# Attention and 32 experts on one core: experts scatter weighted rows by token and choice instead of tokens gathering them

## The chip, the core and the metric

The kernel runs on one core of a Trainium2 chip. Its engines are TensorE (PE; the loads of its weights are PEld), VectorE (DVE), ScalarE (ACT), GpSimd (POOL) and SyncE (SP), which here only issues DMAs. The metric is device time in microseconds; lower is better. The kernel before took 1311.79 us, the median of three runs (1309.03 to 1314.77).

## What is computed

The input x has 8 sequences of 512 tokens with 128 channels, so N = 4096 tokens. A layer of causal attention (16 heads of 64, one null key and value for each head) is followed by a residual sum and a layer norm; the result is x1. Then comes a mixture of E = 32 experts, of which each token takes K = 4, and again a residual sum and a layer norm:

```python
w, idx = _gate(xf, wg)                       
fe = idx.reshape(-1)                         
pos = (jnp.cumsum(oh, axis=0) * oh).sum(-1) - 1
keep = pos < cap                             
dest = jnp.where(keep, fe * cap + pos, E * cap)
...
h = jax.nn.silu(jnp.einsum('ecd,edh->ech', xe, w1)) * jnp.einsum('ecd,edh->ech', xe, w3)
out = jnp.einsum('ech,ehd->ecd', h, w2) * buf_w.reshape(E, cap, 1)
y = jnp.zeros((N + 1, DIM), x.dtype).at[buf_tok].add(out.reshape(E * cap, DIM))[:N]
z = jax.nn.silu(xf @ sw1) * (xf @ sw3) @ sw2
return (y + z).reshape(shape)
```

There are 16384 choices and 20480 slots (32 x 640). A choice beyond the 640th of its expert is dropped; slots that nobody takes stay empty. Everything is float32.

## The kernel before

**Attention.** 64 steps, one for each sequence and pair of heads (g = 8 b + p). A step computes scores in four rounds of 128 queries (L462, two heads), adds the mask and takes the row minimum of the negated scores on VectorE (L472, into ns and nm), takes the exponential with its row sum on ScalarE (L482, into pr), and finishes with `normalize` (L488 to L501): on POOL pn is prepared (L492), ScalarE takes its exponential (L493), POOL adds it to the sums (L495), VectorE takes the reciprocal (L496), and POOL multiplies pr by it (eight L500). Two steps later pr is transposed on PE (L510; the copies out of PSUM are L515 on ScalarE and L517 on VectorE) and multiplied by v (L528; its copy yT is L536). The pool ps_m has four PSUM buffers; transposes, projections and outputs take turns on them. Score tiles have two buffers for each head.

**Routing.** When the eight pairs of a sequence are done, `finish` and `route` for this sequence are put piece by piece into the following steps: output projection (L257), norm (L283), transposed copy of x1 (L292, ScalarE), gate (L298), choice of groups and experts, positions by a product with a triangular matrix (L389, L390), and from these the slot of each choice, gidx (L403). Then `dispatch` issues 16 indirect DMAs for the sequence (L407, on POOL), one for each of 4 tiles and 4 choices. Each scatters 128 rows of 512 bytes from x1_all to their slots in xe_d in HBM. At the start SP's queue fills xe_d with zeros (L432).

The framework that builds the kernel tracks tiles: since all scatters write xe_d, each waits for the one before it to land. It also sets the order of the instructions on each engine, by its own schedule, within these dependencies. What is issued by POOL runs in that order, scatters and arithmetic alike.

**Experts.** The shared expert (L600 to L615) fills acc with x1 + z. Then for each of the 32 experts: SP loads its slots (xe, L625) and weights (L586), PE transposes five tiles of 128 slots (L633), multiplies by w1 and w3 (L600, L602) and w2 (L660), and SP stores the 320 KB result oe to oe_d (L668). The weights wait for the combination.

**Combination.** For each of 32 tiles of tokens and each of the four choices POOL gathers 128 rows of 512 bytes from oe_d (L678), and VectorE adds weight times row to acc (L684). After four tiles the layer norm's statistics are complete; POOL computes rstd (L691, L692), VectorE applies it (L695), and SP stores the result.

Of the kernel before, what the change touches and what calls it, by code (L numbers as in the profile page):

```python
# [17 lines left out]
P = 128  # L18
# [5 lines left out]
def attn_moe_kernel(  # L24
# [41 lines left out]
    xe_d = dram.tile([NSLOT, C], F32, name="xe_d")  # L66
    oe_d = dram.tile([NSLOT + 1, C], F32, name="oe_d")
# [3 lines left out]
    w_all = keep.tile([P, NTT, K], F32, name="w_all")  # L71
# [36 lines left out]
    zeros = const.tile([P, C], F32, name="zeros")  # L108
    nc.gpsimd.memset(zeros, 0.0)

# [7 lines left out]
    wat = astack.enter_context(tc.tile_pool(name="wat", bufs=1))  # L118
    ps_s = astack.enter_context(tc.tile_pool(name="ps_s", bufs=2, space=PSUM))
# [148 lines left out]

    def rstd_of(mv, name):
# [5 lines left out]
    def route(b, seq):  # L275
# [69 lines left out]

        def experts():
# [3 lines left out]
            for t in range(NT):  # L350
# [9 lines left out]
                w_all[:, t0 : t0 + NT, :], ev[:, :, :K], tot.unsqueeze(2).broadcast_to([P, NT, K]), ALU.mult  # L360
# [44 lines left out]
        def dispatch(t):  # L405
            for k in range(K):
                nc.gpsimd.indirect_dma_start(  # L407
                    out=xe_d[:, :],
                    out_offset=bass.IndirectOffsetOnAxis(ap=gidx[:, t0 + t, k : k + 1], axis=0),
                    in_=x1_all[:, t0 + t, :],  # L410
                    in_offset=None,
                    bounds_check=NSLOT - 1,
                    oob_is_err=False,
                )
# [4 lines left out]
        yield groups  # L419
        yield experts  # L420
# [10 lines left out]
    for z in range(0, NSLOT, P * ZR):  # L431
        nc.sync.dma_start(  # L432
            xe_d[z : z + P * ZR, :].rearrange("(p r) c -> p r c", r=ZR),
            zeros.unsqueeze(1).broadcast_to([P, ZR, C]),
        )
    nc.sync.dma_start(oe_d[NSLOT : NSLOT + 1, :], zeros[0:1, :C])
# [186 lines left out]
    def load_slots(e):  # L623
        xe = ework.tile([P, NJ, C], F32, tag="xe", name=f"xe_{e}")
        nc.sync.dma_start(xe, xe_d[e * CAP : (e + 1) * CAP, :].rearrange("(p j) c -> p j c", j=NJ))  # L625
        return xe

    def transpose_slots(e, xe):
        xeT = ework.tile([P, CAP], F32, tag="xeT", name=f"xeT_{e}")
        for j0, j1 in ((0, 4), (4, NJ)):  # L630
            px = ps_x.tile([P, 512], F32, tag="x", name=f"px_{e}_{j0}")
            for j in range(j0, j1):
                nc.tensor.transpose(px[:, (j - j0) * P : (j - j0 + 1) * P], xe[:, j, :], ident)  # L633
# [9 lines left out]
    for e in range(E):  # L643
# [4 lines left out]
        if e + 1 < E:  # L648
            xeTs[e + 1] = transpose_slots(e + 1, xes.pop(e + 1))
# [7 lines left out]
        for j0, j1 in ((0, 4), (4, NJ)):  # L657
# [5 lines left out]
            dst = oe[:, j0:j1, :].rearrange("p j c -> p (j c)")  # L663
            if j0 == 0:
                nc.scalar.copy(dst, po[:, : (j1 - j0) * C])
            else:
                nc.vector.tensor_copy(dst, po[:, : (j1 - j0) * C])
# [64 lines left out]
```

## Time and profile before

| | us |
|---|---|
| median of three runs | 1311.79 |
| the profiled execution, its own time | 1315.74 |
| its span on the core | 1314.0 |
| first slots to last slots scattered for the last sequence | 939.9 to 982.2 |
| first transpose of expert 0 | 986.3 |
| last store of an expert issued | 1120.9 |
| first gather | 1124.3 |
| last normalization ends | 1310.5 |

| engine | busy us | share of the span |
|---|---|---|
| PE | 1007.1 | 77% |
| DVE | 650.1 | 49% |
| ACT | 567.5 | 43% |
| POOL | 588.9 | 45% |

How to read it: the page divides the span into 40 equal slices (32.9 us each) and gives the busy share of each engine in tenths, 9 being 90% or more. A group's row has the line, the engine, the operation, the tiles it writes and reads, the number of instructions, then the busy time, the mean of one in ns, and the idle time of the engine just before them with what ended most of it. A timeline's row has start, duration, engine, line and operation, and in brackets the idle time before it and what ended that. "issue" means that the engine waited for nothing that the profile shows. The granted clock is TensorE's, 1.00 being full speed.

Further rows that the steps use: L407 has a median of 0.992 us and lies between 0.964 and 1.253; L500 takes 0.70 us for 512 columns; L515 0.57; L399 and L615 (128x512, VectorE) 0.69; the statistics L688 and L689 take 0.29 and 0.18; L692 1.04; the store of oe_d lands 2.4 us after its issue; the first slice moves 296 GB/s.

### The profile page before, as it was taken

How to read it: one execution, taken by the hardware profiler on the slowest of the kernel's cores; microseconds unless marked ns; L12 is line 12 of the kernel's file. 1: busy time of each engine (PE TensorE's matmuls, PEld its weight loads, DVE VectorE, ACT ScalarE, POOL GpSimd, SP SyncE). 2: the span in 40 equal slices, each digit the busy share in tenths (PEclk: the TensorE clock that was granted, in tenths of full speed). 3: DMA queues.
4: the chain of work that ended last, by engine and by line, in shares of the span. 5: the costliest groups of instructions: out<-in, count | busy, mean ns of one | idle time of the engine just before them, and what ended most of it. 6: DMA issues, size and time to landing. Idle time of an engine off the chain costs nothing.

```text
span 1314.0 us, 17689 instructions
## 1 busy us (share of the span) xinstructions
PE 1007.1 (77%) x5522; PEld 607.2 (46%) x5522; DVE 650.1 (49%) x2209; ACT 567.5 (43%) x1627; POOL 588.9 (45%) x1047
## 2 busy tenths in 40 slices
PE   6999998989899898999989899998809999100000
PEld 3555654655464464456446445655507777000000
DVE  3655573575557457455645745563604444233323
ACT  3676465546646555564655556553203444000000
POOL 0544356346535634653563465355130000576774
PEclk9999998989899898989989898999858999555555
DMA  9500000000000000000000000000016665121221
GB/s 296 154 1 1 9 13 21 1 11 21 11 9 13 21 1 11 23 9 9 15 18 2 5 21 9 1 14 19 14 32 192 211 211 168 59 65 48 64 59 45
DMA packets 62640, 62.69 MB, mean 48 GB/s; under 512 B 7337, under 2 KB 49746, under 8 KB 62546
## 3 DMA queue, kind: packets, MB, share of 16 engines
q1 hardware_dynamic: 54002, 44.25, 11.1%
q0 software_dynamic: 8192, 16.75, 4.4%
q8 instruction: 44, 0.72, 0.2%
q10 hardware_dynamic: 352, 0.55, 0.1%
q14 instruction: 50, 0.41, 0.1%
HBM read 30.11 MB, written 31.46 MB: 47 GB/s over the span
## 4 chain that ended last, share of the span: by engine, by line
PE 46%; POOL 20%; issue 13%; DVE 10%; DMA 6%; ACT 4%; another core or an unknown queue 1%; POOLq 0%; DVEq 0%; ACTq 0%; SPq 0%
PE y L528 8%; PE s L462 7%; POOL got L678 7%; PE t L510 6%; POOL pr L500 5%; POOL xe_d L407 5%; PE pm_o L257 4%; DMA xe_d<-x_all,gidx 4%; PE o L660 3%; PE pm_v L221 3%; ACT pr L482 3%; PE h L600 3%; PE h L602 3%; DVE ns L472 2%; PE pm_q L204 2%
## 5 line engine op out<-in xcount | busy, mean ns | idle before, releaser
L482 ACT ACTIVATE pr<-ns,nm 128x128 f32<-128x128 f32 (+3 forms) x512 | 283.5, 555 | 183.0 <-DVE nm L472 183.0
L472 DVE CUSTOM_DVE_ANT_0 ns<-s,mask,sn 128x128 f32<-128x128 f32 (+3 forms) x512 | 258.3, 546 | 117.8 <-PE s L462 96.7
L500 POOL TENSOR_SCALAR pr<-pr,tot 128x128 f32<-128x128 f32 (+3 forms) x512 | 265.6, 536 | 26.7 <-DVE tot L496 21.9
L462 PE MATMUL s<-k,q 64*128 64x128 f32 (+3 forms) x1024 | 210.3, 487 | 24.0 <-DVE nm L472 23.2
L678 POOL DMA_INDIRECT got<-oe_d,gidx x128 | 122.7, 959 | 179.0 <-issue 175.4
L528 PE MATMUL y<-prT,v 128*64 128x512 f32 (+3 forms) x1024 | 192.4, 469 | 6.8 <-DVE prT L517 6.8
L407 POOL DMA_INDIRECT xe_d<-x_all,gidx x128 | 129.2, 1009 | 138.5 <-DMA xe_d<-x_all,gidx 115.2
L510 PEld LDWEIGHTS t<-ident,pr 128*128 128x128 f32 x1280 | 141.0, 144 | 107.5 <-issue 55.0
L510 PE MATMUL t<-ident,pr 128*128 128x128 f32 x1280 | 185.7, 285 | 2.2 <-ACT yT L536 1.9
L462 PEld LDWEIGHTS s<-k,q 64*128 64x128 f32 x1024 | 80.9, 189 | 125.5 <-DVE nm L472 62.0
L528 PEld LDWEIGHTS y<-prT,v 128*64 128x64 f32 x1024 | 80.3, 144 | 117.4 <-issue 61.6
L492 POOL TENSOR_TENSOR pn<-nm,sn 128x8 f32<-128x8 f32 x64 | 16.1, 251 | 223.2 <-DVE nm L472 215.9
L515 ACT COPY prT<-t 128x512 f32<-128x512 f32 x192 | 108.6, 566 | 4.3 <-PE t L510 4.0
L482 ACT ACTIVATION_READ_ACCUMULATOR pr<-ns,nm 128x1 f32 x512 | 96.3, 188 | 0.0
L517 DVE COPY prT<-t 128x512 f32<-128x512 f32 x128 | 87.8, 686 | 14.0 <-PE t L510 10.1
L684 DVE SCALAR_TENSOR_TENSOR acc<-got,w_all,acc 128x128 f32<-128x128 f32 x128 | 44.0, 350 | 91.5 <-DMA got<-oe_d,gidx 64.7
L496 DVE RECIPROCAL tot<-tot 128x8 f32<-128x8 f32 x64 | 12.8, 200 | 143.2 <-POOL tot L495 143.2
L536 ACT COPY yT<-y 128x512 f32<-128x512 f32 x64 | 37.3, 583 | 104.5 <-PE y L528 104.5
L210 PE MATMUL pm_k<-xT,wk_sb 128*128 128x512 f32 x128 | 71.8, 645 | 2.2 <-ACT prT L515 1.7
L221 PE MATMUL pm_v<-wv_sb,xT 128*128 128x256 f32 x256 | 67.8, 395 | 0.0
L204 PE MATMUL pm_q<-xT,wq_sb 128*128 128x512 f32 x128 | 66.1, 598 | 2.0 <-ACT v L228 2.0
L257 PEld LDWEIGHTS pm_o<-wo_sb,yT 128*128 128x128 f32 x512 | 61.9, 192 | 7.8 <-issue 6.7
(133 smaller groups left out, 1126.2 us busy)
## 6 DMA issues: line engine op xcount, KB each, us to landing
xe_d<-zeros SPq DMA_DIRECT2D x8, 1280.0 KB, 11.4
xe<-xe_d SPq DMA_DIRECT2D x32, 320.0 KB, 3.4
oe_d<-oe SPq DMA_DIRECT2D x32, 320.0 KB, 2.4
w<-in_L_ffn_w_dram SPq DMA_DIRECT2D x96, 64.0 KB, 2.4
xn<-in_L_attn_x_dram SPq DMA_DIRECT2D x8, 256.0 KB, 4.8
xe_d<-x_all,gidx POOLq DMA_INDIRECT x128
got<-oe_d,gidx POOLq DMA_INDIRECT x128
out_dram<-ot SPq DMA_DIRECT2D x8, 256.0 KB, 2.3
```

What stands on the lines that cost most here:

```text
L204: nc.tensor.matmul(pm, wq_sb[:, p * P : (p + 1) * P], s["xT"], start=True, stop=True)
L221: nc.tensor.matmul(pm[:, t * 2 * P : (t + 1) * 2 * P], s["xT"][:, r * P : (r + 1) * P], wv_sb[:, c * 2 * P : (c + 1) * 2 * P], start=True, ...
L257: nc.tensor.matmul(pm[:, :C], s["yT"][p][:, rows], wo_sb[:, p, :], start=(p == 0), stop=False)
L407: nc.gpsimd.indirect_dma_start(out=xe_d[:, :], out_offset=bass.IndirectOffsetOnAxis(ap=gidx[:, t0 + t, k : k + 1], axis=0), in_=x1_all[:, ...
L462: nc.tensor.matmul(ps[e][:, :n], st["q"][e * D : (e + 1) * D, i * P : (i + 1) * P], st["k"][e * D : (e + 1) * D, :n], start=True, stop=True,)
L472: nc.vector.tensor_tensor_reduce(out=ns[:, :n], in0=ps[e][:, :n], in1=mask[:, T - n :], scale=1.0, scalar=s["sn"][:, i, 2 * p + e : 2 * p ...
L482: nc.scalar.activation(st["pr"][:, e, row0[i] : row0[i] + n], ns[:, :n], AF.Exp, bias=st["nm"][:, i, e : e + 1], scale=-1.0, accum_out=st[ ...
L500: nc.gpsimd.tensor_scalar(cols, cols, tot[:, i, e : e + 1], 1.0, ALU.mult, ALU.mult)
L510: nc.tensor.transpose(pt[:, k * P : (k + 1) * P], st["pr"][:, e, row0[i] + j * P : row0[i] + (j + 1) * P], ident)
L515: nc.scalar.copy(dst, pt)
L528: nc.tensor.matmul(yp[e * D : (e + 1) * D, j * P :], v[:, j, c0 : c0 + D], st["prT"][:, e, col0[j] : col0[j] + n], start=(j == 0), stop=(j ...
L678: nc.gpsimd.indirect_dma_start(out=got, out_offset=None, in_=oe_d[:, :], in_offset=bass.IndirectOffsetOnAxis(ap=gidx[:, n, k : k + 1], axi ...
```

## The change

Rows in xe_d grow from 128 to CE = 132 floats: behind the channels they carry the choice's own number (token x 4 + choice, as an integer) and its weight. ScalarE builds these rows in a new tile xk (four copies for each sequence), POOL writes the number, VectorE the weight. An empty slot carries a number that is out of bounds. The scatters of the dispatch are declared independent of each other, and the loads of xe get explicit dependencies on them.

The experts multiply by the weight when they copy out of PSUM: VectorE now takes the four-tile part, ScalarE the one-tile part. The store of oe is replaced by five indirect DMAs on POOL for each expert, which scatter 128 rows of 512 bytes each to y_d, at the row that the slot carries; out of bounds rows are not written. These too are declared independent. y_d is filled with zeros at the start. The combination waits for all of them, loads four contiguous rows for each token (1 MB for each group of four tiles), and adds them and acc; for every second group the widest add runs on POOL.

```diff
+    CE = C + 4
+    NOWHERE = 0x7F000000
+    xe_d = dram.tile([NSLOT, CE], F32, name="xe_d")
+    y_d = dram.tile([N * K, C], F32, name="y_d")
...
+    nc.gpsimd.memset(empty[:, C : C + 1].bitcast(I32), NOWHERE)
+    place = const.tile([P, NTT, K], I32, name="place")
+    nc.gpsimd.iota(place, pattern=[[P * K, NTT], [1, K]], base=0, channel_multiplier=K)
...
+    xkp = astack.enter_context(tc.tile_pool(name="xkp", bufs=1))
...
+    scatters = {"slots": [], "choices": []}
+
+    def apart(group, dma):
+
+        tc.declare_no_dep(dma.ins, group=group, reason="rows of its own")
+        tc.add_to_no_dep_group(group, dma.ins)
+        scatters[group].append(dma.ins.name)
+
+    def after(group, dma):
+
+        for name in scatters[group]:
+            tc.add_manual_dep(
...
+        def rows():
+
+            g["rows"] = xk = xkp.tile([P, NT, K, CE], F32, tag="xk", name=f"xk_{b}")
+            for t in range(NT):
+                nc.scalar.copy(
+                    xk[:, t, :, :C], x1_all[:, t0 + t, :].unsqueeze(1).broadcast_to([P, K, C])
+                )
+            nc.gpsimd.tensor_copy(xk[:, :, :, C].bitcast(I32), place[:, t0 : t0 + NT, :])
+            nc.gpsimd.memset(xk[:, :, :, C + 2 :], 0.0)
...
-                w_all[:, t0 : t0 + NT, :], ev[:, :, :K], tot.unsqueeze(2).broadcast_to([P, NT, K]), ALU.mult
+                g["rows"][:, :, :, C + 1], ev[:, :, :K], tot.unsqueeze(2).broadcast_to([P, NT, K]), ALU.mult
...
-                nc.gpsimd.indirect_dma_start(
-                    out=xe_d[:, :],
-                    out_offset=bass.IndirectOffsetOnAxis(ap=gidx[:, t0 + t, k : k + 1], axis=0),
-                    in_=x1_all[:, t0 + t, :],
...
+                apart(
+                    "slots",
+                    nc.gpsimd.indirect_dma_start(
+                        out=xe_d[:, :],
+                        out_offset=bass.IndirectOffsetOnAxis(ap=gidx[:, t0 + t, k : k + 1], axis=0),
+                        in_=g["rows"][:, t, k, :],
...
         yield groups
+        yield rows
         yield experts
...
-            zeros.unsqueeze(1).broadcast_to([P, ZR, C]),
+            empty.unsqueeze(1).broadcast_to([P, ZR, CE]),
         )
-    nc.sync.dma_start(oe_d[NSLOT : NSLOT + 1, :], zeros[0:1, :C])
+    ZR = 16
+    for z in range(0, N * K, P * ZR):
+        nc.sync.dma_start(
+            y_d[z : z + P * ZR, :].rearrange("(p r) c -> p r c", r=ZR),
+            zeros[:, :C].unsqueeze(1).broadcast_to([P, ZR, C]),
+        )
...
-        xe = ework.tile([P, NJ, C], F32, tag="xe", name=f"xe_{e}")
-        nc.sync.dma_start(xe, xe_d[e * CAP : (e + 1) * CAP, :].rearrange("(p j) c -> p j c", j=NJ))
+        xe = ework.tile([P, NJ, CE], F32, tag="xe", name=f"xe_{e}", bufs=5)
+        after("slots", nc.sync.dma_start(xe, xe_d[e * CAP : (e + 1) * CAP, :].rearrange("(p j) c -> p j c", j=NJ)))
...
-            if j0 == 0:
-                nc.scalar.copy(dst, po[:, : (j1 - j0) * C])
+            w = xes[e][:, j0:j1, C + 1 : C + 2]
+            if j1 - j0 == 1:
+                nc.scalar.activation(oe[:, j0, :], po[:, :C], AF.Copy, scale=w[:, 0, :])
             else:
-                nc.vector.tensor_copy(dst, po[:, : (j1 - j0) * C])
-        nc.sync.dma_start(oe_d[e * CAP : (e + 1) * CAP, :].rearrange("(p j) c -> p j c", j=NJ), oe)
+                nc.vector.tensor_tensor(
+                    oe[:, j0:j1, :],
+                    po[:, : (j1 - j0) * C].rearrange("p (j c) -> p j c", c=C),
+                    w.broadcast_to([P, j1 - j0, C]),
+                    ALU.mult,
+                )
+        xe = xes.pop(e)
+        for j in range(NJ):
+            apart(
+                "choices",
+                nc.gpsimd.indirect_dma_start(
+                    out=y_d[:, :],
+                    out_offset=bass.IndirectOffsetOnAxis(ap=xe[:, j, C : C + 1].bitcast(I32), axis=0),
+                    in_=oe[:, j, :],
+                    in_offset=None,
+                    bounds_check=N * K - 1,
+                    oob_is_err=False,
+                ),
+            )
...
+    y_t = y_d.rearrange("(n p k) c -> p n (k c)", p=P, k=K)
     for n0 in range(0, NTT, NT):
+        got = ework.tile([P, NT, K * C], F32, tag="got", name=f"got_{n0}", bufs=4)
+        after("choices", nc.sync.dma_start(got, y_t[:, n0 : n0 + NT, :]))
+        two = ework.tile([P, NT, 2 * C], F32, tag="two", name=f"two_{n0}", bufs=2)
+        half = nc.vector if (n0 // NT) % 2 == 0 else nc.gpsimd
+        half.tensor_tensor(two, got[:, :, : 2 * C], got[:, :, 2 * C :], ALU.add)
+        nc.vector.tensor_tensor(two[:, :, :C], two[:, :, :C], two[:, :, C:], ALU.add)
+        nc.vector.tensor_tensor(acc[:, n0 : n0 + NT, :], acc[:, n0 : n0 + NT, :], two[:, :, :C], ALU.add)
...
-            for k in range(K):
-                got = ework.tile([P, C], F32, tag="got", name=f"got_{n}_{k}", bufs=16)
-                nc.gpsimd.indirect_dma_start(
-                    out=got,
-                    out_offset=None,
-                    in_=oe_d[:, :],
-                    in_offset=bass.IndirectOffsetOnAxis(ap=gidx[:, n, k : k + 1], axis=0),
-                )
-                nc.vector.scalar_tensor_tensor(
-                    acc[:, n, :], got, w_all[:, n, k : k + 1], acc[:, n, :], ALU.mult, ALU.add
-                )
```

In the instruction order of the two builds, POOL's 16 scatters of a sequence stood in clumps of one to four among the instructions of `normalize` before, and stand in one row of 16 after; from the ninth on each waits for the one eight before it. On VectorE the reciprocal of the pair that follows them stood ahead of the next step's first two L472 before and stands behind them after. The pool of xk has one buffer; oe keeps three, xe gets five.

## The prediction

> **What bounds the kernel now.** I read the page's slices first, then its costliest groups, then the timelines of the stages that these point to. Slices 1 to 28 are attention, 29 and 30 the end of the dispatch, 31 to 34 the experts, 35 to 40 the combination.
>
> ```profile
> PE   6999998989899898999989899998809999100000
> ...
> POOL 0544356346535634653563465355130000576774
> ...
> L678 POOL DMA_INDIRECT got<-oe_d,gidx x128 | 122.7, 959 | 179.0 <-issue 175.4
> ...
> L407 POOL DMA_INDIRECT xe_d<-x_all,gidx x128 | 129.2, 1009 | 138.5 <-DMA xe_d<-x_all,gidx 115.2
> ...
> L496 DVE RECIPROCAL tot<-tot 128x8 f32<-128x8 f32 x64 | 12.8, 200 | 143.2 <-POOL tot L495 143.2
> ```
>
> PE is full in attention and in the experts and idle behind them: the last 190 us (1124.3 to 1314.0) belong to POOL's 128 gathers. Both indirect kinds hold POOL for about a microsecond each. The scatters also wait for one another (115.2 us), and VectorE waits for POOL (143.2 us, at the reciprocal of the softmax sums).
>
> POOL's timeline gives the two paces. First the last sequence's scatters, with nothing beside them, then gathers of the tail:
>
> ```profile
> 958.65 0.97 POOL L407 DMA_INDIRECT xe_d<-x_all,gidx  x1 [1.53 <-DMA xe_d<-x_all,gidx]
> 961.16 0.97 POOL L407 DMA_INDIRECT xe_d<-x_all,gidx  x1 [1.54 <-DMA xe_d<-x_all,gidx]
> ...
> 1143.07 0.94 POOL L678 DMA_INDIRECT got<-oe_d,gidx  x1 [0.30 <-issue]
> 1144.32 0.94 POOL L678 DMA_INDIRECT got<-oe_d,gidx  x1 [0.30 <-issue]
> ```
>
> A chained scatter takes 2.51 us (0.97 on POOL, 1.54 until it has landed). An unchained gather takes 1.25 (0.94 and a gap of 0.30). So an unchained scatter should take 0.97 + 0.30 = 1.27.
>
> What POOL's scatters do to attention is seen on PE's timeline in the middle of a batch:
>
> ```profile
> 670.76 1.02 PE L204 MATMUL pm_q<-xT,wq_sb 128*128 128x512 f32 x2
> 675.35 1.92 PE L462 MATMUL s<-k,q 64*128 64x384 f32 x4 [3.56 <-DVE nm L472]
> 677.19 1.11 PE L510 MATMUL t<-ident,pr 128*128 128x128 f32 x4
> 678.10 1.91 PE L210 MATMUL pm_k<-xT,wk_sb 128*128 128x512 f32 x2
> 679.94 2.08 PE L462 MATMUL s<-k,q 64*128 64x512 f32 x4
> 681.95 1.09 PE L510 MATMUL t<-ident,pr 128*128 128x128 f32 x8
> ```
>
> VectorE stood 8.19 us at the reciprocal, since four scatters were ahead of it on POOL; PE stood 3.56 us. Then PE ran at half speed: the four groups from 675.35 to 681.95 took 6.60 us, and the same four a step earlier 3.35, so 3.25 were lost as well. The clock row by stage shows the same (granted 0.93 from 178.8 to 230.0, 1.00 from 60.0 to 126.7).
>
> **The change, part by part.** The sum is against the profiled execution: 1315.74 us, of which 1314.0 are span. It lies 3.95 above the median of the runs, 1311.79; I take the difference over to the median.
>
> *Attention, sequences 0 to 6.* The chain between scatters goes: in the built order each waits only for the one eight before it. But the scheduler now issues all 16 of a sequence in a row, where they stood before in clumps of one to four between the normalizations. I follow sequence 4's times. The slots are ready at 637.4; 16 x 1.27 hold POOL until 657.7. The head pair behind them needs POOL (L492), ScalarE's exponential, POOL (L495) and VectorE's reciprocal, by their rows 1.5 us: 659.2. ScalarE stands at that exponential and VectorE at that reciprocal, which the new order puts behind two ns of the next step; that step's scores start at 645.9. PE can go on through two rounds of scores, eight transposes, a q, a third round and four transposes: by the rows from 645.9 to 650.0. Then PE lacks a PSUM buffer, because ScalarE has not copied the first transposes. ScalarE must first do four pr (0.4 to 0.5 and 0.19 each) and that copy (0.57), so PE resumes at about 661.9. It stands 11.9 us and then loses the 3.25 at half speed: 15.2. What the clumps cost before: from the five yT copies after the slots, the steps of sequence 0 take 9.82, 13.72, 14.95, 12.61 and 10.68, and without a dispatch 9.82, 11.16, 10.68, 11.16 and 10.68, so 8.3. Net +7.0 for each of seven sequences: **+49**. Bounds: if nothing of the clump reaches PE, -8.3 each; if all of the 20.3 does, with the slow clock, +15.
>
> *Rows that carry destination and weight.* Four ScalarE copies (128x512, 0.57 by the row of L515) for each sequence. ScalarE has a gap of 1.33 us just there; three of the four come ahead of the x1T copy, on which PE already waits 1.1 us. I take 0.4 x 8 = **+3**. POOL's small writes are issued in its idle time. Zeroing y_d adds eight stores of 1 MB on SP's queue, ahead of the experts' weights and the fourth sequence's x; these are needed from 290 us on, the fills end near 100, and the first scatter waits for them only at 180: nothing. If that cover were gone, 8.4 MB at the 296 GB/s of the first slice are 28 us.
>
> *Dispatch of the last sequence.* It is on the path: 939.9 to 982.2. Unchained 16 x 1.27 - 0.3 = 20.0: **-22**.
>
> *Experts.* Now 4.07 us each, PE full (granted clock 1.00 from 995 to 1116). Behind each expert POOL gets five scatters in place of SP's one store: 5 x 1.28 = 6.4 us (a little over 1.27, since scatters beside VectorE have a median of 0.99). POOL becomes the bound. From the first transpose to the first store are 8.9 us, with the wider multiply 9.2; then 160 x 1.28 = 204.8; then 1.5 until the last has landed: 215.5, against 137.9 from the same point to the first gather: **+78**. Three oe and five xe buffers give two experts' slack, so that POOL doesn't starve: expert e may write its oe once the scatters of e-3 have landed, some 12 us ahead of its turn. Behind that wait stand VectorE's and ScalarE's work for the next expert, behind the reload of xe on SP the next weights; both are then early by the same slack. The multiply takes VectorE's 0.69 in place of 0.29, beside POOL. Bounds of one scatter: 0.97 + 0.17 (the smallest gap) = 1.14 and 1.06 + 0.30 = 1.36, the far end 2.51.
>
> [...]
>
> *Combination.* 128 gathers, 128 multiply-adds and eight stops for rstd go (189.7 us). In their place come eight 1 MB loads, which wait for all scatters; behind them on SP are only the output stores. First landing: 1.05 MB at 296 GB/s is 3.5, and 2.4 as a 320 KB store takes: 6. VectorE then has for each group of four tiles two adds of 512 (0.69 each by L399), eight statistics (2.1), four normalizations (1.2), and in every second group the wide add (1.4): 43 in all; the last rstd on POOL adds 1.5, fill 1.5: 46. The other seven loads (25 us) lie beside it, as do POOL's four wide adds (at least 1.4 by L500). After the last normalization come 3.5, as now. 6 + 46 + 3.5 = 55.5 against 189.7: **-134**. Bounds 45 and 70.
>
> Sum: 49 + 3 - 22 + 78 - 134 = -26, and with the roundings -27: 1289 in that execution, **1285** by the median.
>
> **Rivals.**
> 1. *The clump costs attention no more than the scattered ones did.* PE has run ahead before: 8.19 us of VectorE's standing cost it only 3.56. Then the 49 go and 1236 is left (1178, if nothing of it reaches PE). Against it: ScalarE is held too, and PSUM has four buffers of that kind.
> 2. *The scatter is slower among the experts* (the slower side). The place is POOL's 160 scatters; the price is 160 us for each microsecond. It decides at (1312 - 1285) / 160 = 0.17 over 1.28, that is 1.45. At 1.6 the kernel takes 1336, at the chained 2.51 (if the declared independence did not hold) 1482. For it: rows grow and their source is read beside VectorE and ScalarE; two such gathers took 1.09. Against it: the built order shows waits eight back, and gathers beside VectorE held 1.25.
> 3. *PE stays at half speed among the experts.* It would be busy 4.07 of 6.4 us. At half speed it needs up to 8.1: 32 x 1.7 = 54 more, 1339. It decides above 7.2 us for an expert. Against it: pauses are 2.3 us, and a PE that is slow is always busy, which in this trace ends the slow state after 6.6 us.
>
> On this the row above shows the half speed after a pause of 3.56 us. [...]
>
> **How the numbers follow.** Forecast 0.56, 1260 to 1308 by the near bounds; first rival 0.14 (1236, with 0.03 of it wholly hidden); second 0.16 (over 1311); third 0.06; the clump's full price (15 in place of 7, 1341) 0.08. The range 1236 to 1324 reaches to the first rival and into the slower ones. Over 0.5% is 6.6 us, about what a measurement can tell from no change. Faster: nearly all of the forecast, the first rival and a little of the third, 0.71; same 0.08; slower 0.21.
>
> **What would show it.** Scatters among the experts 1.25 to 1.30 apart and POOL full there; PE idle 10 to 13 us once in each sequence, released through ScalarE; the last sequence's scatters 1.27 apart; about 55 us from the last scatter to the end. I would be wrong if scatters came 1.45 apart or more, if PE showed no such pauses, or if loads or adds stretched the end beyond 70 us.

## The result, and the profile after

The changed kernel takes **1327.17 us** (median of five runs, 1322.64 to 1330.39), beside 1311.79 for the kernel before (1309.03 to 1314.77). The ratio is 1.0118 [1.0086, 1.0151]: 1.2% longer, which is clear of the noise but under 2%, where 1285 and a range of 1236 to 1324 were forecast.

From the profile's page of the changed kernel, the slices and three of the costliest groups:

```profile
PE   6999987996999699879969996997884666676500
...
POOL 0534355426433643554274346435414666666633
PEclk9999998987998799989879997989886878778855
...
L722 POOL DMA_INDIRECT y_d<-oe,xe x160 | 155.4, 971 | 95.8 <-issue 53.3
...
L445 POOL DMA_INDIRECT xe_d<-xk,gidx x128 | 125.8, 983 | 70.8 <-issue 38.2
...
L541 DVE RECIPROCAL tot<-tot 128x8 f32<-128x8 f32 x64 | 13.0, 203 | 139.2 <-issue 64.4
```

The row of nines that PE had in attention is broken by a 6 or 7 once per sequence. The experts are slices 32 to 38 in place of four, with PE at 5 to 7 and POOL at 6, not at the 7 or 8 that scatters 1.28 apart would give (0.97 / 1.28 = 0.76). The tail is two slices in place of six. The scatters of the dispatch (L445) no longer wait for each other, and a scatter among the experts holds POOL for 0.971 us, one of the dispatch for 0.983.

The profiled execution took 1330.39 us (span 1328.6), the one before 1315.74 (1314.0). By the stages of the two timelines:

| stage | before | after | difference | forecast |
|---|---|---|---|---|
| start to the last sequence's first scatter | 939.9 | 992.9 | +53.0 | +49 + 3 |
| that sequence's dispatch | 42.3 | 22.0 | -20.3 | -22 |
| from its last scatter to the end of the experts' stage | 142.1 | 252.6 | +110.5 | +78 |
| from there to the end of the span | 189.7 | 61.2 | -128.5 | -134 |
| sum | 1314.0 | 1328.6 | +14.6 | -27 |

The cuts are at 939.9, 982.2 and 1124.3 (the first gather) before, and at 992.93, 1014.88 and 1267.45 (the last scatter has landed) after. Of the miss of about 41 us, 32.5 are in the experts.

**The clump in attention** is as the prediction drew it. A timeline of the changed kernel, end of a row of 16 scatters:

```profile
692.06 0.97 POOL L445 DMA_INDIRECT xe_d<-xk,gidx  x1 [0.30 <-issue]
693.30 0.21 ACT L538 ACTIVATE pn<-pn 128x8 f32<-128x8 f32 x1 [12.13 <-issue]
693.82 0.20 DVE L541 RECIPROCAL tot<-tot 128x8 f32<-128x8 f32 x1 [10.63 <-issue]
...
695.50 1.22 PE L218 MATMUL pm_k<-xT,wk_sb 128*128 128x512 f32 x1 [10.76 <-DVE prT L562]
```

POOL comes to the normalization only after its last scatter; ScalarE has stood 12.13 us by then and VectorE 10.63; PE, which waits for a copy out of PSUM behind them, 10.76.

**In the experts** the surprise is visible at PE's results. The changed kernel's timeline, with the columns start, duration, engine, line and, in brackets, the idle time before it and what ended that:

```profile
1030.40 0.94 PE L705 MATMUL o<-w,hT 128*128 128x128 f32 x6
1031.15 0.69 DVE L712 TENSOR_TENSOR oe<-o,xe 128x512 f32<-128x512 f32 x1 [0.81 <-issue]
...
1035.71 0.94 PE L705 MATMUL o<-w,hT 128*128 128x128 f32 x6 [1.23 <-issue]
...
1039.43 0.97 POOL L722 DMA_INDIRECT y_d<-oe,xe  x1 [0.30 <-issue]
...
1041.49 0.69 DVE L712 TENSOR_TENSOR oe<-o,xe 128x512 f32<-128x512 f32 x1 [5.83 <-remote]
1041.53 0.37 ACT L710 ACTIVATE oe<-o,xe 128x128 f32<-128x128 f32 x1 [7.42 <-remote]
...
1042.17 0.97 POOL L722 DMA_INDIRECT y_d<-oe,xe  x1 [1.77 <-issue]
```

VectorE's group over all 32 experts:

```profile
L712 DVE TENSOR_TENSOR oe<-o,xe 128x512 f32<-128x512 f32 x32 | 22.1, 691 | 112.5 <-remote 63.9 <-PE h L645 19.4 <-PE o L705 9.9
```

At 1031.15 VectorE takes PE's result o at once. The next o is done at 1036.65 at the latest by PE's records, but VectorE and ScalarE start on it at 1041.5, 4.8 us later. "remote" says that nothing in the profile released them. The moment is telling: POOL's last scatter before the pause left it at 1040.40, and 1.1 us later, when a scatter lands (its semaphore is raised at 1041.50), both results arrive. Then POOL, which had run dry, starts again: a gap of 1.77 us. It is no single case: of VectorE's 17 oe that come over 1.5 late, 15 start 1.03 to 1.22 us after POOL's last scatter ended.

The trace also records the semaphores, counters that one engine's instructions raise and another's wait for. PE's, on which this oe waits, is raised at 1035.08 and then not before 1041.46, though eight matmuls that raise it have ended by their records in between; the DMA that this oe waited for as well had landed at 1022.49. And it is the third expert's oe in three buffers, so no earlier scatter held it. What ended the wait was PE's late signal.

I call a result late by the time from the later of two moments to its consumer's start: the recorded end of the matmul that the consumer waits for, and the end of its engine's instruction ahead (for oe also the landing of the scatters that held its buffer, for VectorE's L649 the end of ScalarE's L648, whose result it multiplies). The usual value is 0.04 to 0.15, the largest of the kernel before 0.48. After the change 61 of the experts' 256 results are over 0.5 late, the latest 7.4. The scatters are 1.276 apart where they follow each other, as forecast, but 19 gaps, one for about every second expert, hold 34.2 us. With them the mean spacing is 1.49.

**In the tail** a timeline of the changed kernel shows two of the eight groups' ends, without and with POOL's wide add beside them:

```profile
1279.96 1.11 DVE L753 TENSOR_SCALAR ot<-acc,mv,rstd 128x128 f32<-128x128 f32 x4 [0.94 <-POOL rstd L750]
...
1286.29 2.34 POOL L740 TENSOR_TENSOR two<-got 128x1024 f32<-128x1024 f32 x1
1286.35 3.13 DVE L753 TENSOR_SCALAR ot<-acc,mv,rstd 128x128 f32<-128x128 f32 x4 [1.24 <-POOL rstd L750]
```

Four normalizations take 3.13 us beside POOL's add and 1.11 otherwise.

### The profile page after: what moved, and what is told of

Read it like the earlier page. It is cut to its first block, busy times and chain, and to the rows that moved or that the text cites. A ratio compares the mean times of both kernels' runs of the same rounds, so it can differ in the third digit from the quotient of the medians.

```text
span 1328.6 us, 18045 instructions
## 1 busy us (share of the span) xinstructions
PE 1050.8 (79%) x5522; PEld 639.2 (48%) x5522; DVE 641.4 (48%) x2101; ACT 576.1 (43%) x1659; POOL 626.5 (47%) x1102
## 4 chain that ended last, share of the span: by engine, by line
PE 59%; issue 14%; DVE 8%; another core or an unknown queue 6%; POOL 5%; ACT 5%; DMA 2%; SPq 0%; POOLq 0%; DVEq 0%; ACTq 0%
PE y L573 12%; PE s L507 11%; PE t L555 9%; PE pm_o L265 4%; PE pm_v L229 4%; PE pm_q L212 4%; PE pm_k L218 3%; ACT pr L527 3%; PE o L705 3%; DVE ns L517 2%; PE h L647 2%; PE h L645 2%; POOL pr L545 2%; PE px L678 1%
## 5 line engine op out<-in xcount | busy, mean ns | idle before, releaser
L545 POOL TENSOR_SCALAR pr<-pr,tot 128x128 f32<-128x128 f32 (+3 forms) x512 | 262.0, 531 | 26.5 <-DVE tot L541 20.3
L507 PE MATMUL s<-k,q 64*128 64x128 f32 (+3 forms) x1024 | 214.1, 484 | 12.8 <-DVE tot L541 9.8
L573 PE MATMUL y<-prT,v 128*64 128x384 f32 (+3 forms) x1024 | 198.6, 469 | 5.0 <-DVE prT L562 3.6
L722 POOL DMA_INDIRECT y_d<-oe,xe x160 | 155.4, 971 | 95.8 <-issue 53.3
L445 POOL DMA_INDIRECT xe_d<-xk,gidx x128 | 125.8, 983 | 70.8 <-issue 38.2
L573 PEld LDWEIGHTS y<-prT,v 128*64 128x64 f32 x1024 | 84.6, 144 | 109.9 <-issue 55.2
L218 PE MATMUL pm_k<-xT,wk_sb 128*128 128x512 f32 x128 | 72.9, 654 | 64.9 <-DVE prT L562 54.0
L705 PE MATMUL o<-w,hT 128*128 128x128 f32 x320 | 63.6, 343 | 72.0 <-DVE hT L649 46.9
L562 DVE COPY prT<-t 128x512 f32<-128x512 f32 x128 | 87.9, 687 | 19.6 <-PE t L555 19.4
L581 ACT COPY yT<-y 128x512 f32<-128x512 f32 x64 | 37.5, 585 | 137.1 <-PE y L573 122.9
L705 PEld LDWEIGHTS o<-w,hT 128*128 128x128 f32 x320 | 53.5, 240 | 89.0 <-DVE hT L649 52.9
L712 DVE TENSOR_TENSOR oe<-o,xe 128x512 f32<-128x512 f32 x32 | 22.1, 691 | 112.5 <-remote 63.9
L710 ACT ACTIVATE oe<-o,xe 128x128 f32<-128x128 f32 x32 | 11.7, 367 | 148.4 <-remote 76.5
```

Source lines behind the costliest of these rows:

```text
L218: nc.tensor.matmul(pm, wk_sb[:, p * P : (p + 1) * P], s["xT"], start=True, stop=True)
L445: nc.gpsimd.indirect_dma_start(out=xe_d[:, :], out_offset=bass.IndirectOffsetOnAxis(ap=gidx[:, t0 + t, k : k + 1], axis=0), in_=g["rows"][ ...
L507: nc.tensor.matmul(ps[e][:, :n], st["q"][e * D : (e + 1) * D, i * P : (i + 1) * P], st["k"][e * D : (e + 1) * D, :n], start=True, stop=True,)
L545: nc.gpsimd.tensor_scalar(cols, cols, tot[:, i, e : e + 1], 1.0, ALU.mult, ALU.mult)
L562: nc.vector.tensor_copy(dst, pt)
L573: nc.tensor.matmul(yp[e * D : (e + 1) * D, j * P :], v[:, j, c0 : c0 + D], st["prT"][:, e, col0[j] : col0[j] + n], start=(j == 0), stop=(j ...
```

## The experiments

The kernels of a group ran on one chip; I: e1 to e4, II: e5 to e8, III: e9 to e12, IV: e13 to e16, V: e17 and e18. The record numbers these chips 6, 0, 1, 8 and 0 again. Before on them took 1301.62, 1312.77, 1315.41, 1316.5 (one run) and 1297.7. Where no other base is named, a diff is against the changed kernel.

### Group I: buffers, pace, chain, plain stores

The first theory (A) was that PE's results are late because of the scatters beside them; rival B was that the buffers of oe and xe run out.

**e1, more buffers.**

```diff
-        xe = ework.tile([P, NJ, CE], F32, tag="xe", name=f"xe_{e}", bufs=5)
+        xe = ework.tile([P, NJ, CE], F32, tag="xe", name=f"xe_{e}", bufs=8)
-        oe = ework.tile([P, NJ, C], F32, tag="oe", name=f"oe_{e}")
+        oe = ework.tile([P, NJ, C], F32, tag="oe", name=f"oe_{e}", bufs=6)
```

> Six buffers for oe in place of three and eight for xe in place of five; nothing else. In the profile of the changed kernel POOL stands 1.5 to 2.2 us longer than its usual 0.30 ahead of about every second expert's first scatter, about 34 us over 32 experts. Theory A: these gaps come from TensorE's results reaching VectorE and ScalarE late (up to 7 us after the matmul's end) while a row of independent scatters runs on POOL; buffers do not help, the gaps stay within 34 +- 8 us, and the time stays at 1318 to 1330. Theory B: the gaps come from oe and xe buffers that are released by the scatters' landing; with more of them the gaps go, and the time is about 1327 - 34 = 1293.

Measured: 1291.83 (1291.57 to 1295.8), 0.9929 [0.9904, 0.9954]. POOL has no gaps, the experts take 218.3 (1014.89 to 1233.14, when the last scatter has landed). Groups of the trace of e1:

```profile
L712 DVE TENSOR_TENSOR oe<-o,xe 128x512 f32<-128x512 f32 x32 | 22.1, 692 | 26.3 <-PE o L705 19.4 <-DMA y_d<-oe,xe 7.0
...
L722 POOL DMA_INDIRECT y_d<-oe,xe x160 | 155.5, 972 | 61.5 <-issue 33.5 <-ACT xeT L682 13.0 <-DMA y_d<-oe,xe 9.1
```

VectorE now waits for PE's o and never for "remote". By itself this speaks for B; but no result is late in attention either (in its rows of 16 the changed kernel had 17), where e1 changes nothing. So the run could also owe it to the chip or the time at which it ran, and that had to be tried again (e5, e7).

**e2, a pause between scatters:** a multiply of 128x256 on POOL ahead of each scatter of the experts.

```diff
+        op = nc.gpsimd.tensor_scalar(idle, idle, 1.0, None, ALU.mult)
...
         for j in range(NJ):
+            pause()
             apart(
```

> Ahead of each of the experts' 160 scatters POOL does one multiply of an idle 128x256 tile. POOL's L500 took 0.70 us for 512 columns in the kernel before, so some 0.4 us each, and a scatter every 1.7 to 1.8 us instead of 1.28: 160 x 0.45 = 72 us more on POOL. Theory A1 (the lateness of TensorE's results depends on the rate of the scatters): no result comes more than 0.5 us late, the gaps between the experts go, and the time is about 1327 + 72 - 34 = 1365. Theory A2 (it depends on how many independent scatters have run since POOL's last pause, about seven): results are late by several us as before, gaps stay, 1395 to 1405. Theory B (buffers) says nothing on lateness.

Measured: 1428.26, 1.0964 [1.0919, 1.1009]. No result is late, but none was late in e1 and e3 either. The pause cost more than thought: the spacing is 2.11, not 1.7 to 1.8, and 160 x 0.83 = 133 us.

**e3, the dispatch of sequences 0 to 6 chained again,** the last one's left independent.

```diff
-                apart(
+                (apart if b == B - 1 else lambda group, dma: scatters[group].append(dma.ins.name))(
```

> The dispatch of sequences 0 to 6 is chained again (each scatter waits for the one before it to land, as in the kernel before, and the built order spreads them again in clumps of one to three); the last sequence's 16 scatters stay independent. In the profile the last sequence's first scatter starts at 992.9 against 939.9 before. Theory C (the clumps of 16 on POOL cost this): it starts at 940 to 946, and the time is 1327 - 50 = 1277. Rival (the four row copies on ScalarE and the filling of y_d cost it): it stays near 990 and the time near 1325.

Measured: 1254.29 (1249.36 to 1264.7), 0.9619 [0.9575, 0.9663], 37.5 less than e1 on its chip. In the profiled run, the longest of the four, the last sequence's first scatter comes at 960.9, not at 940 to 946, against 992.94 in e1. So the clump in attention costs more than the whole change loses, and a chain that spreads the scatters between normalizations is worth it. e3 has the three and five buffers of the changed kernel, and here POOL has no gaps among the experts either, which speaks against B already.

**e4, plain stores** in place of the experts' scatters.

```diff
-                nc.gpsimd.indirect_dma_start(
-                    out=y_d[:, :],
...
+                nc.gpsimd.dma_start(
+                    y_d[(e * NJ + j) * P : (e * NJ + j + 1) * P, :], oe[:, j, :]
```

> The experts' five scatters are plain stores of the same 64 KB, issued by POOL as well and independent as well, to consecutive rows of a longer y_d: this kernel leaves out that each row goes to its own place. Theory A-indirect (TensorE's results are late only beside indirect DMAs): no result is over 0.5 us late, no gaps; if a plain store holds POOL as long as a scatter (1.28), the time is about 1293, and less if it holds it shorter. Theory A-any (late beside any row of DMAs that POOL issues): late by several us, gaps as before, 1327 at the same spacing.

Measured: 1217.13, 0.9352 [0.931, 0.9393]. That is 75 less than e1: about what 160 indirect scatters cost over 160 stores where no result is late (e4 has the smaller buffers).

### Group II: the same kernel again, and the dispatch spread out

**e5, the changed kernel unchanged.**

> The changed kernel itself, unchanged, beside kernels of its own kind. Before took 1301.6 in the last experiments, where no result of TensorE came late in the runs with more buffers and with chained dispatch, 1311.8 when the changed kernel was timed. Theory A-place (the late results belong to the chip or the moment in which the changed kernel was timed, not to the kernel): if before takes some 1300 again, no result is over 0.5 us late, the gaps on POOL are gone with the three and five buffers that it has, and the time is that of the run with more buffers, 1292 (0.993 of before). Theory B (more buffers removed the gaps): gaps of about 34 us again, 1.0118 of before.

Measured: 1329.23 (1327.13 to 1333.02), 1.0129 [1.01, 1.0157]. 61 late results, gaps of 37.2, and 17 late in attention. The loss comes back.

**e6, the dispatch spread:** single scatters, each ordered behind the last POOL instruction of the normalization ahead of it, four behind each of four.

```diff
+        if group == "slots" and len(normalized) < B * NP:
+            tc.add_manual_dep(
+                dma.ins,
+                normalized[-1],
+                mybir.DependencyInfo(mybir.DependencyClass.NoSync, mybir.DependencyReason.DATA),
...
-            yield lambda t=t: dispatch(t)
+            for k in range(K):
+                yield lambda t=t, k=k: dispatch(t, k)
```

> All scatters of the dispatch stay independent, but for sequences 0 to 6 four of them are ordered behind each of four normalizations, in place of 16 in a row. Four scatters take 5.1 us of POOL, a step's normalization about 4.9, a step 10.7 to 11.2. Theory C (the row of 16 is what stretches attention): the last sequence's first scatter comes at 940 to 950 (992.9 in the changed kernel, 960.9 with the chain), and the time is the changed kernel's of the same chip less 43 to 53. Rival D (POOL then has no room, and each of these steps stretches as with the chain): 960, and the changed kernel's time less 32.

Measured: 1245.31 (1240.66 to 1248.26), 0.9498 [0.9464, 0.9532]; the last sequence's first scatter comes at 899.7. The time is 84 less than that of e5, where 43 to 53 were expected. Windows from 135 to 240 us, a sequence with its dispatch: first of the kernel before, then of the changed one, then of e6. The columns are length, busy time of PE, PEld, DVE, ACT and POOL with their instructions, granted clock, DMA share and GB/s.

```profile
135.00:240.00 105.00, 96.35 (x530) 54.56 (x529) 58.68 (x212) 57.78 (x170) 53.15 (x103) 0.95 0.04 14
```

```profile
135.00:240.00 105.00, 90.97 (x515) 53.60 (x514) 55.71 (x204) 55.95 (x163) 49.67 (x99) 0.93 0.04 14
```

```profile
135.00:240.00 105.00, 101.73 (x585) 59.13 (x584) 64.34 (x232) 65.42 (x190) 56.46 (x113) 1.00 0.04 14
```

In the same 105 us e6 gets 585 matmuls done, before 530, after 515, and only in e6 is the granted clock 1.00. The five steps behind the slots take 53.51 on average, against 61.40 before, 67.32 after, and 53.50 where there is no dispatch: spread like this, scatters cost attention nothing. The clump's 13.8 (67.32 - 53.50) goes whole, and not only down to the 7.9 (61.40 - 53.50) of the kernel before, as expected.

**e7, the same with the buffers of e1.**

> The same with six oe and eight xe buffers. Theory A-place: equal to the spread dispatch alone within 4 us where no result of TensorE is late, since POOL is full there with three and five buffers too. Theory B: faster than the spread dispatch alone by some 30.

Measured: 1245.69, 0.9491 [0.9457, 0.9524]. POOL's gaps hold 33.4 us, 69 results are late. A group of the trace of e7:

```profile
L722 DVE TENSOR_TENSOR oe<-o,xe 128x512 f32<-128x512 f32 x32 | 22.1, 691 | 96.9 <-remote 48.8 <-PE h L655 12.5 <-PE o L715 9.9
```

Twice the buffers and still "remote": rival B falls. What was different in e1 was not its buffers.

**e8, e7 with all wide adds on VectorE** (`half = nc.vector`).

> The same, and VectorE does the wide add of every group. In the changed kernel the end, from the last scatter's issue to the last instruction, took 62.5 us, and four normalizations 3.13 beside POOL's wide add (2.34) against 1.11 otherwise. If the two engines slow each other, four wide adds of 1.22 on VectorE (4.9) replace three times 2.0 (6.1) and VectorE's waits for POOL (about 1.2 at each of four): 3 to 6 us shorter than without. If not, 2 to 5 us longer.

Measured: 1236.96 (1232.21 to 1242.32), 0.9415 [0.9377, 0.9453]. From the end of POOL's last scatter the tail takes 59.6 against 62.2 in e7, so 2.6 are the adds'. The other 6 are not shown to be: attention ended at other times in the two profiled runs (897.4 and 909.9 for the first scatter).

### Group III: how much is the dispatch alone, and is it the rate

**e9, the kernel before with a spread, independent dispatch** and nothing else of the change.

```diff
+        last = nc.gpsimd.tensor_tensor(pn, pn, tot, ALU.mult)
+        normalized.append(last.ins.name)
...
-        nc.sync.dma_start(xe, xe_d[e * CAP : (e + 1) * CAP, :].rearrange("(p j) c -> p j c", j=NJ))
+        after("slots", nc.sync.dma_start(xe, xe_d[e * CAP : (e + 1) * CAP, :].rearrange("(p j) c -> p j c", j=NJ)))
```

> The kernel before with one change: its dispatch's scatters are independent and ordered four by four behind the normalizations, as in the spread kernel; rows, experts and combination are those of before. Theory (most of the spread kernel's gain comes from the dispatch, not from the experts' scatters): the last sequence's first scatter comes at about 900 in place of 939.9 and its 16 take 22 in place of 42.3, so 60 us less: 0.954 of before. Rival (the gain needs the experts' side): 0.98 to 1.00.

Measured: 1244.1 (1241.17 to 1246.39), 0.947 [0.9423, 0.9516]. The slices of e9, then of e6:

```profile
PE   5999989999999998999999899998859997000000
...
POOL 0534358428626734743663574274220001776774
```

```profile
PE   5999999999999999999999999988847667667400
...
POOL 0444347436634842762573375355055666656633
```

e9 keeps the experts in four slices (three nines and a 7) and the six slices of gathers; e6 has eight slower slices of experts and two of tail. Both are at 0.95: where results come late, weights and scatters in the experts bring no gain that these intervals (about half a per cent each way) could tell, and the gain of e6 is the dispatch's.

**e10, the changed kernel on this chip** (one run, as e11 to e16).

> The changed kernel once more, one look: it tells whether TensorE's results are late beside its experts' scatters where the next two kernels run. On the chip of the second experiments they were (up to 7.05 us, gaps of 37 us), on that of the first they were not with the same experts' part.

Measured: 1334.97, 62 late, gaps of 43.4.

**e11, a small pause** (a 128x1 memset on POOL ahead of each scatter).

> The changed kernel with a 128x1 memset on POOL ahead of each of the experts' scatters, so that they come 1.5 to 1.8 us apart in place of 1.28. Theory A1 (lateness depends on the rate): where the changed kernel's results are late, these are late less often or not at all (gaps under 10 us). Theory A2 (it depends on the number of scatters since POOL's last pause): gaps of 30 to 40 us again.

Measured: 1341.71. The spacing stayed at 1.28, since the memset (0.13) fits into the 0.30 that POOL stands between scatters anyway; 62 late. It tells nothing of the rate by itself, but it shows that this instruction on POOL between scatters didn't help. A group of its trace:

```profile
L734 DVE TENSOR_TENSOR oe<-o,xe 128x512 f32<-128x512 f32 x32 | 22.1, 692 | 93.0 <-remote 45.9 <-issue 13.8 <-PE h L669 13.8
```

**e12, the pause of e2 again, on a chip with late results.**

> A scatter every 2.11 us, as in the earlier run of this kernel, where only the last two experts' results were late (one by 8.1 us). Theory A1: the same here, gaps under 10 us. Theory A2: where the changed kernel's results are late, these are too, by several us from the sixth or seventh scatter on.

Measured: 1427.26. At a spacing of 2.11 none of the 256 is late (longest 0.4), though 20 are in the same run's rows of 16 in attention, where scatters follow each other at 1.27. (The two late results that the expectation gives to e2 were waits for scatters that held oe's buffer; counted as above, e2 has none.) A group of the trace of e12:

```profile
L734 DVE TENSOR_TENSOR oe<-o,xe 128x512 f32<-128x512 f32 x32 | 22.1, 692 | 168.1 <-PE o L727 141.1 <-issue 15.9 <-DMA y_d<-oe,xe 11.1
```

So 160 scatters without a pause make nothing late at this spacing: of the two forms of theory A that were set against each other, the rate (A1) holds, and a long unbroken run alone (A2) doesn't do it.

### Group IV: what of a scatter does it

**e13, narrow rows:** 64 bytes of each row into a tensor of their own.

```diff
-                    out=y_d[:, :],
+                    out=part_d[:, :],
-                    in_=oe[:, j, :],
+                    in_=oe[:, j, :16],
```

> The experts' scatters write rows of 64 bytes in place of 512, to a tile of their own; this kernel leaves out that the experts' outputs reach the combination. The number of rows, their indices and the spacing of 1.28 us stay. If the bytes make TensorE's results late: on a chip with late results in the dispatch's rows of 16 none in the experts, gaps under 5 us, some 1295. If the number of rows or POOL's rate does: late by several us, gaps of 30 to 45 us, 1327 to 1335.

Measured: 1345.23; 55 late, gaps of 46.5. **e14, gathers** of 128 rows in the scatters' place (`out=sink[i % 16]`, `in_=y_d[:, :]`).

> In the place of each of the experts' scatters stands a gather of 128 rows of 512 bytes from y_d into a tile that nobody reads; it waits for ScalarE's part of oe as the scatter did. This kernel leaves out that the experts' outputs reach the combination. The gathers of the kernel before came 1.25 us apart. If indirect DMAs at this rate make the results late whichever way they move: late by several us, gaps of 30 to 45 us. If only writing does: none late by over 0.5 us, gaps under 5 us.

Measured: 1334.2; spacing 1.25, 53 late, gaps of 41.6. **e15, plain stores** as in e4.

> The experts' plain stores on POOL's queue again, for the case that this chip has late results: on the chip of the first experiments, which had none, five of them took POOL 2.65 us and TensorE set the pace, 4.07 us for each expert. If any DMA of POOL's makes results late: over 0.5 us late at several experts, and an expert takes over 4.2 us. If not: 4.07 us again, and 1217 times this chip's before over 1301.6.

Measured: 1220.35; none late (longest 0.2), though 21 are in attention. **e16, a medium pause** (a 128x384 memset).

> A 128x384 memset on POOL ahead of each of the experts' scatters. The 128x1 memset was hidden in the 0.30 us between scatters; this one should bring them to 1.5 to 1.8 us apart. Theory A1 (rate): fewer late results than at 1.28, gaps under 15 us. If the limit lies above this spacing: gaps of 30 to 45 us again.

Measured: 1345.0; spacing 1.57, none late (longest 0.1), POOL's gaps 1.6 in all; 21 late in attention. But 160 x 0.29 = 47 is more than the gaps that it saves. One group of each trace, in the order e13, e14, e15, e16:

```profile
L713 DVE TENSOR_TENSOR oe<-o,xe 128x512 f32<-128x512 f32 x32 | 22.1, 692 | 92.9 <-remote 60.9 <-PE o L706 20.1 <-issue 4.9
```

```profile
L730 DVE TENSOR_TENSOR oe<-o,xe 128x512 f32<-128x512 f32 x32 | 22.1, 692 | 93.5 <-remote 52.8 <-issue 18.0 <-PE o L723 15.8
```

```profile
L722 POOL DMA_DIRECT2D y_d<-oe x160 | 85.0, 538 | 55.9 <-ACT xeT L682 49.7 <-ACT oe L710 3.5 <-DVE hT L649 2.5
```

```profile
L734 DVE TENSOR_TENSOR oe<-o,xe 128x512 f32<-128x512 f32 x32 | 22.1, 692 | 88.2 <-DMA y_d<-oe,xe 42.2 <-PE o L727 32.4 <-PE h L669 5.6
```

An eighth of the bytes and the other direction leave "remote" where it was; plain stores (0.53 of POOL) and a wider spacing take it away. But the plain stores come five in a row and then POOL waits for the next expert; an unbroken row of them was not tried.

### Group V: a version that beats both

**e17 and e18: e8 with a small pause,** a memset of 128x128 and 128x200 ahead of each scatter of the experts.

> The kernel with the spread dispatch, six oe and eight xe buffers and all wide adds on VectorE, with a 128x128 memset (0.20 us in the profile) on POOL ahead of each of the experts' scatters: the 128x384 memset made 1.57 us between scatters, so this should make some 1.35. If lateness begins below 1.35: no result over 0.5 us late in the experts, no gaps, and on a chip with late results 160 x 0.07 = 12 us more and 44 less than without, about 1205 or 0.92 of before (without: 1237, 0.9415). If it begins between 1.35 and 1.57: late results again, 0.94 to 0.95.

> The same with a 128x200 memset, some 1.42 us between scatters. If lateness begins below 1.42: no late results, 160 x 0.14 = 23 us more and 44 less than without, about 1216 or 0.927 of before. If 1.35 is already free of late results, this one is slower by some 11 us than that; if 1.35 still has them and this one has none, it is faster.

Measured: e17, spacing 1.36, 1216.92 (1216.76 to 1225.13), 0.9374 [0.934, 0.9408]; e18, spacing 1.42, 1227.65, 0.9448 [0.9414, 0.9481]. Of the 11 between them 160 x 0.06 = 10 are the spacing. Neither has late results, but neither can show what e8 would have had here: with the dispatch spread there are no rows of 16 left that would tell. The kernel before took 1297.7 beside them and 1312.77 in group II, on what the record calls the same chip, 0. So it is not shown that late results belong to a chip; they may belong to a time. The spacing from which results come in time stays open between 1.28 and 1.57, and so does whether the pause of e17 gains over e8, whose ratio's interval overlaps. e17 is the fastest kernel here that leaves nothing out.

### All together

| kernels | spacing | late of 256 | longest | POOL's gaps | late in attention |
|---|---|---|---|---|---|
| after, e5, e10, e11 | 1.28 | 61 to 62 | 6.3 to 7.4 | 34 to 49 | 17 to 18 (after, e5, e11) |
| e6, e7, e8 (dispatch spread) | 1.28 | 62 to 77 | 5.6 to 6.8 | 33 to 44 | no rows of 16 |
| e13, narrow rows | 1.28 | 55 | 6.4 | 46.5 | 20 |
| e14, gathers | 1.25 | 53 | 6.2 | 41.6 | 19 |
| e16, e12, paused | 1.57, 2.11 | 0 | 0.1, 0.4 | 1.6, 1.1 | 21, 20 |
| e15, plain stores | - | 0 | 0.2 | - | 21 |
| e1, e3 (group I) | 1.28 | 0 | 0.1, 0.2 | 0 | 0 (e1) |
| e2 (group I) | 2.11 | 0 | 0.4 | 1.1 | 0 |
| e4, plain stores (group I) | - | 0 | 0.2 | - | 0 |
| e17, e18 (group V) | 1.36, 1.42 | 0 | 0.1 | 1.8 | no rows of 16 |

The rows down to e15 are from the first measurement and groups II to IV, where results come late in attention or in the experts; the last four are from groups I and V, where none does. In attention's rows of 16 they come 0.7 to 1.0 late in the changed kernel (up to 2.3 in e15 and e16), 8 to 10 us into a row, and cost nothing: the last first scatter is at 992.93 in the changed kernel and at 992.94 in e1.

## Why the prediction was wrong

**The step that failed** is "Three oe and five xe buffers give two experts' slack, so that POOL doesn't starve". It covered late buffers; what came late were PE's results. In the first measurement and in groups II to IV, where indirect DMAs followed each other at 1.25 to 1.28, consumers of PE got up to 7.4 us late what PE's records show as done; in the changed kernel PE and the experts' chain stopped with them, and POOL ran dry for 34.2 us. That the rate decides where results come late is shown by e12 and e16 (none late at 2.11 and 1.57) against e10 and e11 (62 late at 1.28; e11 has a memset between scatters too, but the old spacing); that it is neither bytes nor direction nor buffers by e13, e14 and e7 (55, 53 and 69 late). Of each of these but e7 there is one run. **What stays open** is the path inside the chip. PE's ends are modelled in the trace, so I can't tell a result that PE finishes late from one that is announced late. Also open is why group I has no late results at all, chip or time, and where between 1.28 and 1.57 they end.

For planning, the measurement decides: an indirect DMA beside PE was not free here, with 61 results over 0.5 us late and 34.2 us of gaps in the changed kernel.

By the prediction's own steps:

- **Attention, +49 and +3: the mechanism right, the sum in part by luck.** Measured +53.0. Of it 3.4 are the start, which the prediction had at nothing (PE's first two pm_q matmuls take 2.05 us, before 1.10; why is not shown), 35.5 the clumps of six sequences (67.32 - 61.40 = +5.9 for the five steps of each, forecast +7.0), 6.6 the steps with the row copies (forecast 3) and 7.5 what is left at the last clump. So the clumps cost 43.0 in place of 49, and the start and the row copies happen to make up for it. PE stands 9.8 to 11.0 once in each sequence; 11.9 was the estimate. It goes on after VectorE's copy L562 (54.0 of the 64.9 us that it stands before L218), not after ScalarE's, as the prediction had it.
- **Last dispatch, -22: right**, -20.3; the scatters are 1.28 apart, but for the first two, which are 3.1 apart.
- **Experts, +78: the pace right, the cover wrong.** 1.276 and 0.971 as forecast, but +110.5: the gaps' 34.2 on top. e1, without late results, takes 218.3 between the same points, the forecast 220.
- **Combination, -134: mis-sized by 5.5.** -128.5, with 61.2 left for 55.5. VectorE's normalizations beside POOL's add are about the whole of it: three such groups at 3.13 - 1.11 make 6.1. The prediction had put POOL's adds "beside" VectorE's work at no cost.
- **Rivals.** The first and the price of a full clump did not occur. The second had the place, the price and the point right: its threshold was 1.45 for a mean spacing, and that is 1.49 with the gaps. Its mechanism was not: the scatters themselves stay at 0.971 and 1.276. Of the third only a consequence is seen. Windows of the changed kernel, experts, then tail:

```profile
1014.90:1267.40 252.50, 165.20 (x736) 127.24 (x736) 72.81 (x128) 44.52 (x128) 155.43 (x160) 0.80 0.34 99
1267.40:1328.60 61.20, 0.00 (x0) 0.00 (x0) 38.47 (x116) 0.00 (x0) 21.69 (x20) 0.50 0.52 171
```

The granted clock among the experts is 0.80 and PE is busy 165.2 us, but it stands for the other 87: in e1, with 0.88 among the experts (1028 to 1232 us), POOL keeps the spacing of 1.28 all the same, so the lower clock does not set the pace.

Where and when group I ran, the time would be near the forecast, as far as e1 stands for the changed kernel: e1 takes 1295.8 in its profiled run, forecast 1289, with the combination (61.0 in e1, forecast 55.5) as most of the difference. But the change would still not have given -26 there, since the kernel before takes 1301.62 beside it: 1291.83 - 1301.62 = -9.8. Why the kernel before, too, is about 1% longer in groups II to IV than in I and V has not been found; its trace was taken in neither I nor V, nor was the changed kernel itself run there.

## What to carry to other kernels

Making scatters independent lets a scheduler put them in a row, and a row of 16 held here what its engine owed to others (VectorE stood 10.63 us, ScalarE 12.13, PE 9.8 to 11.0 once in each sequence): order each behind the step's own work (e9: -5%, with one NoSync edge for each, that is an order without a semaphore, and nothing else of the change needed). When indirect DMAs are to run at full rate beside TensorE, don't price them by the engine's own time alone (160 at 1.276 were 204 us here, and the gaps 34.2 more); look for consumers released by "remote", try a spacing between them (none late at 1.57 here, on a chip with 55 at 1.28), and compare on more than one chip and at more than one time, always beside the kernel before. And take a change apart before judging it: this one held a part worth 5% in a form that lost it.

## What was not expected of the hardware

- PE's results up to 7.4 us late beside indirect DMAs 1.25 to 1.28 apart, in the first measurement and groups II to IV only; there none beside plain stores in rows of five (e15), or at spacings of 1.57 and 2.11 (e16, e12).
- A plain store of 64 KB issued by POOL held it for 0.53 us (e15), an indirect one for 0.97 with 0.30 behind it, whether its rows had 512 bytes or 64 (changed kernel, e13).
- Four VectorE normalizations of 128x128 took 3.13 us beside a POOL add of 2.34, and 1.11 without it.
- The kernel before takes 1298 to 1302 us in two of the groups and 1313 to 1317 in three.
